# Order of the matmuls that sum a group of weighted rows: last-made row first, in a graph attention kernel on one Trainium2 core

## The chip, the core and the metric

The kernel runs on one core of one Trainium2 chip. The metric is the device time of an execution in microseconds (us); the time of a kernel is the median over its runs.

## What is computed

A node has 512 features; there are 3327 nodes (padded to 26 tiles of 128) and four layers of graph attention, each on a normalised input and added to it. Cut to one layer, the reference is:

```
h  = relu(layernorm(x)) @ W                      # 3327 x 512, in H heads of 512/H
e  = leaky_relu(s_src[i] + s_dst[j])             # for neighbours j of node i, per head
out_i = sum_j softmax_j(e_ij) * h_j
x  = x + out        (layers 1 and 2: x + elu(out))
```

Heads per layer: 8, 4, 1, 8. The neighbours come from an adjacency matrix with about 17 ones in a row, at most some 36.

## The kernel before

**Stage 0** (to about 317 us of the profiled execution) makes neighbour lists out of the adjacency matrix. Nodes are sorted by number of neighbours, so that tile 0 holds the nodes with most. `CAPS[t]`, 36 for tile 0 down to 11 for tile 25, is the number of neighbour slots of tile t.

**The layers** then work on lists (`tile_gat_lists`). Layer 0 takes all 26 tiles in that way, layer 1 tiles 1 to 25, layer 2 tiles 9 to 25, layer 3 tiles 3 to 25; the remaining tiles of layers 1 to 3, which have most neighbours, are done against all nodes with dense masked products (`Wholes`, L1153, and `Several`, L1301), laid between the list work. Layer l covers 317 to 1102 (l=0), 1130 to 1838 (l=1), 1838 to 2334 (l=2) and 2334 to 2972 us (l=3) of the profiled execution.

A tile's slots are cut into **groups** of up to four (`GROUP`); one group is one **step** s of a layer's list. The order on TensorE (PE), VectorE (DVE), ScalarE (ACT) and GpSimd (POOL) is written out by hand: within a step the pieces run as "first", then the scores of the next step, "scored", then `group` of this step, then "last". The steps of a group are these:

- `fetch` (POOL, L834): one indirect DMA for each slot gathers 128 rows of 528 numbers, each the features and scores of a neighbour, into `g[:, q, :]`. `gpool` has seven buffers, and fetches run up to seven steps ahead. A fetch into a buffer waits until DVE has read the group that was there.
- `scored` (DVE L887, L889, then ACT L890): scores of the four slots and their exponential, into `pw`. It runs one step ahead of `group`.
- `group` (DVE L918, PE L923): DVE multiplies each gathered row by its weights into `m[:, q, :]` (128x512, f32; `mpool` has three buffers), slot after slot. PE then sums the four products by matmuls with the identity matrix into the PSUM tile `self.po` ("bank"; two buffers). The first slot of a tile is not summed by PE: DVE writes its product straight into the bank. In layer 2 (one head) DVE does the sum itself (L911), without PE.
- A tile's last step s is followed by fixed later ones: `divisors` at s, `means` (L941, DVE reads the bank) and `added` (L961) two steps later, then `centre` (ACT L969), `turn` (PE transposes, L450), `cut` (ACT L457), `project` (PE L468), and `rows` (ACT L475 and a DMA of `v` to the table `tab`, from which the next layer gathers). The next layer's first gathers wait for the last of these.

A matmul of f32 appears in the trace as two records of PE, each with a weight load (PEld): 1207 matmuls in L923 are 2414 records. There are 356 groups with matmuls: 225 with four, 66 with three, 44 with two and 21 with one.

Of the kernel before, what the change touches and what calls it, by code (L numbers as in the profile page):

```python
# [795 lines left out]
def tile_gat_lists(ctx: ExitStack, tc: tile.TileContext, x, adj, ws, avs, out, ident, half, slots, L, low, spare, tabx, tabs):  # L796
# [7 lines left out]
    nc = tc.nc  # L804
# [40 lines left out]
    class Tile:  # L845
# [51 lines left out]
        def group(self, i):  # L897


            H, K, wt = HEADS[self.l], CAPS[self.t], self.wt  # L900
            D = F // H
            k0, n, g = self.groups[i]
            if H == 1:
                for q in range(n):
                    v = g[:, q, :].rearrange("p (s m) -> p s m", s=2)[:, :, :F // 2]
                    acc = self.po.rearrange("p (s m) -> p s m", s=2)
                    w = wt[:, k0 + q, 0:1]
                    if k0 + q == 0:
                        nc.vector.tensor_scalar(acc, v, w, None, OP.mult)
                    else:  # L910
                        nc.vector.scalar_tensor_tensor(acc, v, w, acc, OP.mult, OP.add)  # L911
                return
            m = pools["m"].tile([P, GROUP, F], F32, name="m")
            for q in range(n):
                v = g[:, q, :].rearrange("p (s m) -> p s m", s=2)[:, :, :F // 2]

                out_ = self.po if k0 + q == 0 else m[:, q, :]
                nc.vector.tensor_tensor(out_.rearrange("p (s h d) -> p s h d", s=2, d=D),  # L918
                                        v.rearrange("p s (h d) -> p s h d", d=D),
                                        wt[:, k0 + q, :H].rearrange("p (s h) -> p s h", s=2)  # L920
                                        .unsqueeze(3).to_broadcast([P, 2, H // 2, D]), OP.mult)
            for q in range(k0 == 0, n):
                nc.tensor.matmul(self.po, ident, m[:, q, :], start=False, stop=(k0 + q == K - 1),  # L923
                                 skip_group_check=True)

        def divisors(self):
# [542 lines left out]
```

## Time and profile before

| | |
|---|---|
| time, median of 3 runs | 2429.07 us (2425.39 to 2435.29) |
| span of the profiled execution | 2971.7 us, 27155 instructions |
| whole time of the profiled execution | not given beside its span |
| span less median | 542.6 us |
| PE busy | 2211.9 us, of which L923 1232.2 us |
| DVE busy | 1923.1 us, of which L918 into `m` 752.5 us |
| POOL busy | 1731.4 us |
| ACT busy | 934.6 us |
| mean granted clock of PE | 0.873 |

Busy times are from the profiler's records of one execution; a group is named by source line, engine and the tiles it writes and reads (`bank<-m,ident` is L923). "Idle before" is the time in which an engine did nothing ahead of an instruction, put down to whoever released it; "issue" is time for which the profile shows no such reason. The profiled execution took 22% longer than the median of the runs without it, so that its stretches can't be carried over one to one.

### The profile page before, as it was taken

The page shows a single profiled execution, that of the slowest core. Times are in us where ns is not written, and L with a number is a line of the kernel's source. Part 1 is how long each engine was busy: PE and PEld are TensorE (multiplying, and loading weights), DVE is VectorE, ACT ScalarE, POOL GpSimd, SP SyncE. Part 2 cuts the span into 40 slices and gives each one's busy share as a digit, 9 for nine tenths or more (in the row PEclk, how much of TensorE's full clock was granted, in tenths as well). Part 3 has the DMA queues.
Part 4 walks back from the last instruction along what each step waited for, and adds up shares of the span by engine and source line. Part 5 has one row for each costly group of instructions (what it writes and reads, how often), then busy time and mean ns, then how long its engine had stood idle before and what let it go on. Part 6 is the DMA issues. An engine that isn't in the chain of part 4 may idle for free.

```text
span 2971.7 us, 27155 instructions
## 1 busy us (share of the span) xinstructions
PE 2211.9 (74%) x7082; PEld 1246.1 (42%) x7082; DVE 1923.1 (65%) x4968; ACT 934.6 (31%) x2502; POOL 1731.4 (58%) x1717
## 2 busy tenths in 40 slices
PE   4777677776777764767777877588696688878887
PEld 2564233343433332434444444244354454545443
DVE  7987666655565533656665665598888366666665
ACT  5872122322221111322222322244333333323330
POOL 7885455565566635544556562676664556555653
PEclk9988888888898887988888898799898898989888
DMA  6885576786676756755667673787785566656663
GB/s 230 325 291 161 165 228 200 211 254 207 195 225 197 199 130 200 200 157 174 187 190 210 179 209 92 234 255 240 241 246 153 168 193 204 185 170 198 195 189 111
DMA packets 260731, 594.21 MB, mean 200 GB/s; under 512 B 103699, under 2 KB 121107, under 8 KB 256214
## 3 DMA queue, kind: packets, MB, share of 16 engines
q0 software_dynamic: 124368, 432.13, 49.8%
q1 hardware_dynamic: 132454, 153.45, 16.4%
q10 hardware_dynamic: 3744, 6.82, 0.7%
q8 instruction: 57, 0.93, 0.1%
q14 instruction: 108, 0.88, 0.1%
HBM read 542.60 MB, written 49.65 MB: 199 GB/s over the span
## 4 chain that ended last, share of the span: by engine, by line
PE 24%; DVE 18%; issue 14%; another core or an unknown queue 8%; ACT 5%; POOL 3%; DMA 2%; SPq 0%; DVEq 0%; POOLq 0%; ACTq 0%
PE bank L923 16%; DVE m L918 6%; PE pv L468 4%; PE whole L1301 3%; DVE bank L911 3%; POOL g L834 3%; ACT r L1267 1%; DVE z L889 1%; DVE z L887 1%; DVE x L961 1%; PE whole L1153 1%; DMA g<-tab,idxb 1%; DVE em L1126 1%; DVE q L438 1%
## 5 line engine op out<-in xcount | busy, mean ns | idle before, releaser
L923 PE MATMUL bank<-m,ident 128*128 128x512 f32 x2414 | 1232.2, 659 | 335.9 <-DVE m L918 197.3
L918 DVE TENSOR_TENSOR m<-g,pw 128x512 f32<-128x512 f32 x1207 | 752.5, 682 | 384.1 <-ACT pw L890 209.2
L834 POOL DMA_INDIRECT g<-tab,idxb x712 | 678.8, 953 | 482.0 <-issue 197.1
L923 PEld LDWEIGHTS bank<-m,ident 128*128 128x128 f32 x2414 | 488.8, 211 | 942.1 <-issue 582.4
L468 PE MATMUL pv<-w,hT 128*128 128x264 f32 x1664 | 434.9, 416 | 87.8 <-ACT hT L457 61.8
L834 POOL DMA_INDIRECT g<-tabx,twiceb x342 | 324.8, 950 | 230.7 <-issue 147.7
L834 POOL DMA_INDIRECT g<-tab,idxa x297 | 283.7, 955 | 248.4 <-issue 83.9
L468 PEld LDWEIGHTS pv<-w,hT 128*128 128x128 f32 x1664 | 334.1, 205 | 190.3 <-ACT hT L457 68.7
L890 ACT ACTIVATE pw<-z 128x32 f32<-128x32 f32 (+4 forms) x356 | 67.8, 191 | 850.7 <-DVE z L889 484.2
L1153 PE MATMUL whole<-ve,em 128*128 128x512 f32 x468 | 229.4, 642 | 54.1 <-issue 22.9
L1301 PE MATMUL whole<-L,room 128*128 128x130 f32 x1248 | 173.3, 290 | 59.9 <-issue 59.5
L1301 PEld LDWEIGHTS whole<-L,room 128*128 128x128 f32 x1248 | 164.7, 202 | 91.4 <-issue 89.7
L694 POOL TENSOR_TENSOR key<-a,keys 128x3328 int32<-128x3328 int32 (+1 forms) x29 | 189.3, 6530 | 16.3 <-DVE cand L703 11.8
L911 DVE SCALAR_TENSOR_TENSOR bank<-g,L,bank 128x512 f32<-128x512 f32 x243 | 183.3, 754 | 11.1 <-remote 2.0
L1153 PEld LDWEIGHTS whole<-ve,em 128*128 128x128 f32 x468 | 94.0, 206 | 167.4 <-issue 124.5
L834 POOL DMA_INDIRECT g<-tabx,twicea x99 | 94.7, 956 | 104.1 <-issue 51.1
L450 PE MATMUL pt<-ident,xn 128*128 128x128 f32 x416 | 70.8, 298 | 104.7 <-ACT xn L969 60.8
L703 DVE MAX8 cand<-key 128x8 f32<-128x208 int32 x416 | 144.3, 365 | 0.1
L475 ACT ACTIVATE v<-pv,rstd 128x528 f32<-128x528 f32 x78 | 54.2, 694 | 274.4 <-remote 126.5
L1267 ACT ACTIVATE r<-low,L 128x384 f32<-128x384 f32 x208 | 121.2, 583 | 16.9 <-remote 9.5
L918 DVE TENSOR_TENSOR bank<-g,pw 128x512 f32<-128x512 f32 x74 | 51.5, 696 | 100.7 <-ACT pw L890 69.2
L450 PEld LDWEIGHTS pt<-ident,xn 128*128 128x128 f32 x416 | 54.7, 153 | 144.4 <-ACT xn L969 69.1
(180 smaller groups left out, 2195.7 us busy)
## 6 DMA issues: line engine op xcount, KB each, us to landing
a<-in_adj SPq DMA_DIRECT2D x25, 1664.0 KB
tab<-v SPq DMA_DIRECT2D x78, 264.0 KB
ve<-tab SPq DMA_DIRECT2D x78, 264.0 KB
g<-tab SPq DMA_DIRECT2D x65, 264.0 KB
tabx<-vx SPq DMA_DIRECT2D x26, 528.0 KB
g<-tab,idxb POOLq DMA_INDIRECT x712
low<-tab SPq DMA_DIRECT2D x52, 132.0 KB
spare<-tab SPq DMA_DIRECT2D x52, 132.0 KB
```

The costliest lines, as they stand in the source:

```text
L450: nc.tensor.transpose(pt[:, k, :], xn[:, k * P:(k + 1) * P], ident)
L468: nc.tensor.matmul(pv[:, s, :HF + 8], hT[:, k, :], W.w[:, k, s, :], start=(k == 0), stop=(k == KC - 1))
L694: nc.gpsimd.tensor_tensor(key[:, c:c + quarter], a[:, c:c + quarter], keys[:, c:c + quarter], OP.mult)
L703: nc.vector.max(cand[:, g * 8:(g + 1) * 8], key[:, g * SEG:(g + 1) * SEG])
L834: nc.gpsimd.indirect_dma_start(out=out_, out_offset=None, in_=table, in_offset=bass.IndirectOffsetOnAxis(ap=which, axis=0))
L890: nc.scalar.activation(self.wt[:, k0:k0 + n, :H], z, AF.Exp)
L911: nc.vector.scalar_tensor_tensor(acc, v, w, acc, OP.mult, OP.add)
L918: nc.vector.tensor_tensor(out_.rearrange("p (s h d) -> p s h d", s=2, d=D), v.rearrange("p s (h d) -> p s h d", d=D), wt[:, k0 + q, :H].re ...
L923: nc.tensor.matmul(self.po, ident, m[:, q, :], start=False, stop=(k0 + q == K - 1), skip_group_check=True)
L1153: nc.tensor.matmul(tl.po.rearrange("p (s m) -> p s m", s=2), e[:, q * P:(q + 1) * P], v.rearrange("p (s m) -> p s m", s=2)[:, :, :F // 2], ...
L1267: nc.scalar.activation(self.r[:, h, :], self.a[:, g, :], AF.Relu, bias=-1.0, scale=self.b[:, j, g:g + 1])
L1301: nc.tensor.matmul(dst, e[:, h, q * P:(q + 1) * P], mov, start=False, stop=(j == NT - 1), skip_group_check=True)
```

## The change

The matmuls of a group are issued from the highest slot to the lowest. DVE still makes the products from the lowest slot to the highest. The `stop` mark moves to the matmul that now comes last in the tile's last group. Nothing else is changed; lines after L921 move down by one, so that the matmul's line becomes L924.

```
-            for q in range(k0 == 0, n):
-                nc.tensor.matmul(self.po, ident, m[:, q, :], start=False, stop=(k0 + q == K - 1),
+            first = int(k0 == 0)
+            for q in reversed(range(first, n)):
+                nc.tensor.matmul(self.po, ident, m[:, q, :], start=False, stop=(k0 + n == K and q == first),
                                  skip_group_check=True)
```

In the built program the first matmul of a group then waits for DVE's last product, and the others have no wait of their own. Over L923 the matmuls with a wait go from 1207 to 356 and those that signal a semaphore from 1151 to 392; of DVE's products (L918) those that signal go from 1278 to 1013, and those that wait stay 418. All other instructions keep their place on every engine.

## The prediction

> **What bounds the kernel now.** I read the busy times first, then those of each layer, the waits of PE and DVE, and a stretch of the timeline. The three costliest kinds of work are the page's top rows:
>
> ```profile
> span 2971.7 us, 27155 instructions
> ...
> L923 PE MATMUL bank<-m,ident 128*128 128x512 f32 x2414 | 1232.2, 659 | 335.9 <-DVE m L918 197.3
> L918 DVE TENSOR_TENSOR m<-g,pw 128x512 f32<-128x512 f32 x1207 | 752.5, 682 | 384.1 <-ACT pw L890 209.2
> L834 POOL DMA_INDIRECT g<-tab,idxb x712 | 678.8, 953 | 482.0 <-issue 197.1
> ```
>
> The changed matmuls are the largest row of all, and DVE's products are what most often ends PE's idleness. By layer (columns: window, its length, then PE, PEld, DVE, ACT, POOL busy, PE clock, DMA share, GB/s; layers 0, 1 and 3):
>
> ```profile
> 317.00:1102.00 785.00, 570.35 (x1617) 287.50 (x1616) 451.34 (x1189) 172.88 (x457) 455.33 (x479) 0.87 0.71 207
> 1130.00:1838.00 708.00, 542.92 (x1524) 286.56 (x1524) 441.25 (x1182) 195.16 (x595) 375.48 (x396) 0.87 0.63 181
> ...
> 2334.00:2972.00 638.00, 516.91 (x1976) 304.61 (x1976) 407.15 (x796) 195.75 (x610) 352.00 (x370) 0.89 0.63 181
> ```
>
> PE is busiest at 73 to 81%, so none is full. POOL's records hide that after each gather of 0.95 us it takes 0.30 us to issue the next. At 1.25 us a gather, 479, 396 and 370 of them are 600, 495 and 462 us, as much as PE's own 570, 543 and 517. The timeline of a clean stretch shows who sets the pace (start, length, engine, line; in brackets the idle time before):
>
> ```profile
> 928.63 2.48 DVE L918 TENSOR_TENSOR m<-g,pw 128x512 f32<-128x512 f32 x4 [0.33 <-issue]
> ...
> 928.96 0.95 POOL L834 DMA_INDIRECT g<-tabx,twiceb  x1 [0.30 <-issue]
> ...
> 929.37 3.70 PE L923 MATMUL bank<-m,ident 128*128 128x512 f32 x8 [1.08 <-issue]
> ...
> 930.21 0.95 POOL L834 DMA_INDIRECT g<-tabx,twiceb  x1 [0.30 <-issue]
> ```
>
> POOL is back to back, four gathers in 5.0 us. PE was idle for 1.08 us, starts 0.06 us after the first product (DVE makes one every 0.60 us), and runs its four matmuls at 0.86 us each behind the other three. This overlap of DVE and PE within one group is what the change gives up.
>
> ```profile
> PE bank L923 <- DVE m L918: 197.3, 68, 10.3
> ...
> DVE m L918 <- PE bank L923: 19.2, 17, 6.5
> ```
>
> PE waits for products far more than DVE waits for PE to free `m`: PE is usually drained, and DVE seldom blocked.
>
> **What the Trainium skill says.** "Perfetto Trace Analysis", section Tensor Engine Instruction: the end of a matmul's record is estimated, and its semaphore goes out only after PSUM has acknowledged the data. The trace agrees: records are 0.59 us long but start every 0.43 us, so I count starts, not lengths. "TensorE: Matmul & The Clock Gate", section The cost: per-tile semaphore tail: increments of matmuls that end together serialize at 26.3 ns each, and one on the last is enough, since matmuls end in order. No run here shows that price on matmuls that follow each other. The same page, HAM oscillation: gaps of over some 3.4 us drop PE to half clock. The trace shows it: after an idle 8.78 us at 617.9 us the records start every 0.86 us in place of 0.43.
>
> **The change part by part.**
> Waits: 1207 to 356, so 851 fewer. Price: starts of the two records within a matmul lie 429 ns apart (median), and from one matmul to the next, across wait and signal, also 429. A wait already met costs PE nothing: 0, with no gain to be had.
> Signals: 1151 to 392, so 759 fewer. By the same equality 0 on PE; the skill's price would make it at most 759 x 26.3 ns = 20 us, an estimate. I take 0 and keep -20.
> DVE's 265 fewer signals: products start every 598 ns with one and 605 without (three of these). 0.
> Start of a group: it moves from the first product's end to the last's, 3, 2 or 1 times 0.60 us later for four, three or two matmuls. If PE stood idle at each of the 225, 66 and 44 groups: 225 x 1.8 + 66 x 1.2 + 44 x 0.6 = 511 us. Comparing start by start in the trace, 193 of the 356 began before their last product was done, by 233 us together. Even that does not add up: PE takes its queue in order, so once it is 1.8 us late the next group's products are ready sooner relative to it. Shifting PE's rows so, all else held, its delay never passes 1.80 us, and at the ends of layers 0, 1 and 3 it is 0.13, 1.47 and 1.79 us, together +3.4 us. The last tiles have groups of one or two, hence the small first value. That is on the path: the next layer's gathers, or the end, wait for it.
> Behind the waiting matmul stand PE's transposes, projections (L468, 3.56 us) and dense products. Who waits for those? ACT's L475 and L457, with the next exponentials behind them on ACT, and DVE's means. They come two steps after the group, 10 us in a clean stretch, while PE is done 2.48 + 0.06 + 3.43 = 6.0 us after DVE began (4.2 now): 4 us to spare. Where steps bunch after a stall it is not so. I take +3 us for that.
> `m` coming free: slot 0 is now read last, so DVE's first write three groups on may begin 3 x 0.86 = 2.6 us later. On 17 waits that is at most 44 us of DVE idleness; two groups (6.9 us) are then in PE's hands, more than 2.6 + 0.6. At that moment PE hides it: 0. Without this cover it would be lost in full, with gathers behind it, though POOL is six groups ahead.
> No DMA is moved; POOL's and SP's queues keep their order.
> Sum on the profiled execution: 0 + 0 + 0 + 3.4 + 3 = +6 us on a span of 2971.7. The median is 542.6 us lower; the three layer ends are in it just as well, so I carry +6 over: 2435 us.
>
> **The rivals.**
> *Slower: drained hand-overs on the critical chain.* Following the chain of waits, it passes from a product to PE's matmuls at 29 places. For those whose first matmul preceded the last product the delays add to 40 us. If each closes a loop (PE late, ACT late, the next products late), the time is 2429 + 3 + 40 = 2472. It decides once more than some 6 of them count at 1.4 us each, with the layer ends. For it: PE's 197.3 us of waiting. Against: many follow stalls that an unprofiled execution may not have.
> *Faster: signals held up.* The trace has pauses in which PE's semaphores stand still and then arrive in a bunch:
>
> ```profile
> 616.32 0.70 ACT L475 ACTIVATE v<-pv,rstd 128x528 f32<-128x528 f32 x1 [13.36 <-remote]
> ```
>
> ACT waited for a projection recorded as done at 605.7, and PE's updates came at 616.1 to 616.5, 0.04 us apart. I count 64 such bunches, all in layers 0, 1 and 3, about one per 20 signals of PE, none in the 572 us around layer 2, where signals are rare. 542.6 / 64 = 8.5 us is the size of one, which suggests that the profiler makes them; then fewer signals shorten only the profiled execution. If the runs have them too, PE's signals fall by 759 of 2023 executed, 38%. Time with PE, DVE and ACT all idle for over 2 us sums to 210 us; 38% is 80 us, giving 2349.
> *Nothing happens:* the waits really fall, by the built program; but if PE is never drained in a run, its start moves nowhere and 2429 stays.
>
> **How the numbers follow.** Half a per cent (12 us) is about what a measurement can tell from no change. The shift of 3 to 9 us or none: 0.45, own range 2424 to 2441. Loops: 0.33, 2441 to 2480. Held-up signals or the skill's 20 us: 0.22, from 2300 to 2417. For 8 in 10 I reach to 2365 and 2480, leaving out most of the lower tail, about a tenth, and a few in a hundred above.
>
> **What would show it.** In the profile after: the first matmul of a group starts no earlier than 0.05 us after its last product, idleness of PE before it ended by L918 grows beyond 197 us, and spacing within a group stays 0.43 us per record. DVE's waits on PE for `m` stay below some 60 us, else cover has failed. Fewer bunches with an unchanged median says that they are the profiler's; with a median under 2417, that they are real. A median above 2441 says that loops close.

## The result and the profile after

The changed kernel takes 2460.77 us in the median of four runs (2457.97 to 2463.44), against 2430.45 for the kernel before (four runs, 2425.39 to 2435.29): a ratio of 1.0125, interval 1.0108 to 1.0142, so 30 us more. The profiled execution of after has a span of 2461.2 us and a whole time of 2462.9.

The kernel before takes 2430 us at some times and some 2970 at others, without a profile just as with one, and its profile in the prediction is of the second kind. That profile has the pauses in PE's signals that the prediction describes; the profile of after has none. So I set after against the fourth experiment, which takes the same 2430 us as before, has as many waits and signals on PE, and whose profile has no pauses either; I call it **the mirror**. First the rows of the page of after:

```profile
span 2461.2 us, 27155 instructions
...
L924 PE MATMUL bank<-m,ident 128*128 128x512 f32 x2414 | 1127.4, 613 | 155.8 <-DVE m L918 139.5
L834 POOL DMA_INDIRECT g<-tab,idxb x712 | 679.5, 954 | 253.2 <-issue 170.3
L918 DVE TENSOR_TENSOR m<-g,pw 128x512 f32<-128x512 f32 x1207 | 751.8, 681 | 130.1 <-ACT pw L890 126.4
```

and of the mirror, where the matmul's line is L925:

```profile
span 2429.7 us, 27155 instructions
...
L925 PE MATMUL bank<-m,ident 128*128 128x512 f32 x2414 | 1125.3, 614 | 120.1 <-DVE m L918 119.7
```

PE's work is the same to 2 us. DVE's products end 139.5 us of PE's idleness in place of 119.7. The pairs of the waits view for after (us in total, times, longest) add who does not wait:

```profile
PE bank L924 <- DVE m L918: 139.5, 100, 11.8
...
DVE bank L956 <- ACT ex L950: 21.1, 15, 4.1
...
DVE m L918 <- PE bank L924: 2.2, 2, 1.9
```

DVE waits for PE to free `m` for 2.2 us in all. A clean stretch of the timeline of after, in layer 0 (start, length, engine, line; idle time before in brackets), is the counterpart of the prediction's stretch at 928.63:

```profile
741.07 2.48 DVE L918 TENSOR_TENSOR m<-g,pw 128x512 f32<-128x512 f32 x4 [0.27 <-ACT pw L890]
...
743.60 7.13 PE L924 MATMUL bank<-m,ident 128*128 128x512 f32 x16 [0.97 <-DVE m L918]
...
744.15 2.48 DVE L918 TENSOR_TENSOR m<-g,pw 128x512 f32<-128x512 f32 x4 [0.31 <-ACT pw L890]
...
745.05 0.95 POOL L834 DMA_INDIRECT g<-tabx,twiceb  x1 [0.30 <-issue]
```

DVE's four products end at 743.55 and PE begins 0.05 us later, not beside them. Its 16 records are two groups: the second group's products were ready before PE came to them, so of two delays only one shows here.

Cut by layer, from DVE's first product into `m` to the end of its last (layer 2 has no matmul of L923, and is cut at its first and last sum on DVE, L911), the two profiled executions stand so:

| stretch, us | mirror | after | difference |
|---|---|---|---|
| stage 0, to the first product | 310.3 | 303.2 | -7.1 |
| layer 0 | 594.6 | 600.0 | +5.4 |
| from layer 0 to layer 1 | 39.8 | 42.5 | +2.7 |
| layer 1 | 519.6 | 540.4 | +20.8 |
| from layer 1 to layer 2 | 34.3 | 36.8 | +2.5 |
| layer 2 | 417.6 | 417.6 | 0 |
| from layer 2 to layer 3 | 33.1 | 33.0 | -0.1 |
| layer 3 | 469.2 | 474.9 | +5.7 |
| last product to the end | 11.2 | 12.9 | +1.7 |
| span | 2429.7 | 2461.2 | +31.5 |

Stage 0, which the change does not touch, scatters by 9 us between executions (301.4 to 310.3 in the traces of after and experiments 1 to 4), so a single row is good to some us, and the rows below stage 0 add to 38.6 us, more than the 30.3 us of the timed runs; these carry the verdicts. Layer 1 stands out. That the mirror may stand for the kernel before can be seen in experiments 1 to 3: the layers that they leave in the order of before take 595 and 596 us (layer 0), 522 and 521 (layer 1) and 469.2 twice (layer 3) in their traces, within 3 us of the mirror's.

### The profile page after: what moved, and what is told of

The parts are those of the page before. It is cut to its first block, busy times and chain, and to the rows that moved or that the text cites. A ratio compares the mean times of both kernels' runs of the same rounds, so it can differ in the third digit from the quotient of the medians.

```text
span 2461.2 us, 27155 instructions
## 1 busy us (share of the span) xinstructions
PE 2062.4 (84%) x7082; PEld 1181.7 (48%) x7082; DVE 1926.0 (78%) x4968; ACT 932.3 (38%) x2502; POOL 1733.0 (70%) x1717
## 3 DMA queue, kind: packets, MB, share of 16 engines
q1 hardware_dynamic: 132454, 153.45, 19.2%
## 5 line engine op out<-in xcount | busy, mean ns | idle before, releaser
L924 PE MATMUL bank<-m,ident 128*128 128x512 f32 x2414 | 1127.4, 613 | 155.8 <-DVE m L918 139.5
L918 DVE TENSOR_TENSOR m<-g,pw 128x512 f32<-128x512 f32 x1207 | 751.8, 681 | 130.1 <-ACT pw L890 126.4
L924 PEld LDWEIGHTS bank<-m,ident 128*128 128x128 f32 x2414 | 449.9, 195 | 694.6 <-issue 467.1
L468 PE MATMUL pv<-w,hT 128*128 128x264 f32 x1664 | 435.5, 416 | 70.7 <-ACT hT L457 44.7
L468 PEld LDWEIGHTS pv<-w,hT 128*128 128x128 f32 x1664 | 334.7, 205 | 172.8 <-ACT hT L457 51.1
L911 DVE SCALAR_TENSOR_TENSOR bank<-g,L,bank 128x512 f32<-128x512 f32 x243 | 183.2, 754 | 6.8
L1302 PEld LDWEIGHTS whole<-L,room 128*128 128x128 f32 x1248 | 147.5, 190 | 24.9 <-issue 23.7
L1302 PE MATMUL whole<-L,room 128*128 128x130 f32 x1248 | 147.8, 274 | 0.0
L887 DVE TENSOR_TENSOR z<-g,pw 128x32 f32<-128x32 f32 (+4 forms) x356 | 61.8, 174 | 71.5 <-DMA g<-tab,idxa 38.5
L1120 ACT ACTIVATE r<-low,mc,b 128x384 f32<-128x384 f32 x78 | 52.6, 674 | 155.3 <-DVE em L1127 132.3
```

The costliest lines, as they stand in the source:

```text
L468: nc.tensor.matmul(pv[:, s, :HF + 8], hT[:, k, :], W.w[:, k, s, :], start=(k == 0), stop=(k == KC - 1))
L887: nc.vector.tensor_tensor(z, g[:, :n, ROW - 8:ROW - 8 + H], self.s.unsqueeze(1).to_broadcast([P, n, H]), OP.add)
L1302: nc.tensor.matmul(dst, e[:, h, q * P:(q + 1) * P], mov, start=False, stop=(j == NT - 1), skip_group_check=True)
```

## The experiments

Each experiment is compared with the kernel before, timed beside it on the same chip: 2429.99 us for 1 to 4, 2971.1 for 5 to 8, 2969.97 for 9 and 10, 2999.38 for 11 and 2972.46 for 12. So 1 to 4 show what happens without the pauses, 5 to 12 what happens with them. Lines below L921 stand one higher in the experiments than in after (L925 for L924, L1280 for L1279).

### 1 to 3: the reversal in one layer alone

```
-            for q in range(k0 == 0, n):
+            order_ = list(range(int(k0 == 0), n))
+            order_ = order_[::-1] if self.l == 0 else order_     # 1; == 1 in 2, == 3 in 3
+            for q in order_:
```

with the `stop` mark on the last of `order_`. Expected:

> The reversed order in layer 0 alone, the order of before in layers 1 and 3. Theory A (the gathers of POOL pace layers 0 and 3; a late PE costs only where it comes back to stop POOL, and at layer ends): POOL was back to back through nearly all of layer 0 in the profile after, so +3 to +8 us over before. Rival B (every group met by an idle PE loses a bit on a closed loop, evenly): 133 of 356 groups, so 133/356 of 30 us = +11 us. Rival C (reading the buffer or the bank in another order, or fewer signals, is itself slower, whatever the start): also +11 us.

> The reversed order in layer 1 alone. Theory A: layer 1 is the one where POOL stood waiting for DVE (some 33 us between 1054 and 1290 us of the profile after), so most of the 30 us: +15 to +25 us over before. Rivals B and C: 118 of 356 groups, +10 us.

> The reversed order in layer 3 alone. Theory A: POOL had one gap over 0.45 us in all of layer 3 after, so only the end of the layer, +2 to +4 us over before. Rivals B and C: 105 of 356 groups, +9 us.

Measured: layer 0 alone 2433.62 us, ratio 1.0015 (1.0008 to 1.0022), +3.6 us; layer 1 alone 2449.42, 1.0081 (1.0066 to 1.0097), +19.4; layer 3 alone 2437.41, 1.0024 (1.0014 to 1.0035), +7.4. The sum, 30.4 us, is the 30.3 of the whole change: no interaction of the layers shows, and two thirds of the loss lie in layer 1. Layers 0 and 1 came as the expectation's theory A had them. Layer 3 did not: it lost 7.4 us, where A gave it 2 to 4 for the end of the layer and the evenly spread rivals 9. In its trace the stretch of layer 3 itself grows by 6.3 us against the mirror, 2.4 of them at the second groups of tiles and 1.8 at the fifth; what holds these groups was not tested.

Why layer 1? One tile of it in the mirror's timeline:

```profile
1254.15 1.88 DVE L918 TENSOR_TENSOR m<-g,pw 128x512 f32<-128x512 f32 x3
...
1254.88 2.84 PE L925 MATMUL bank<-m,ident 128*128 128x512 f32 x6 [0.90 <-DVE m L918]
...
1257.56 3.72 PE L468 MATMUL pv<-w,hT 128*128 128x264 f32 x16
...
1261.12 0.61 PE L1303 MATMUL whole<-low 128*128 128x129 f32 x4
...
1261.55 0.69 ACT L1280 ACTIVATE low<-low 128x128 f32<-128x128 f32 x2 [0.30 <-PE whole L1303]
...
1264.25 0.69 DVE L957 SCALAR_TENSOR_TENSOR bank<-ex,bank 128x512 f32<-128x512 f32 x1 [1.18 <-ACT ex L951]
...
1266.44 2.48 DVE L918 TENSOR_TENSOR m<-g,pw 128x512 f32<-128x512 f32 x4 [0.25 <-ACT pw L890]
```

and the same tile in the run with layer 1 reversed:

```profile
1259.60 1.88 DVE L918 TENSOR_TENSOR m<-g,pw 128x512 f32<-128x512 f32 x3
...
1261.53 2.84 PE L925 MATMUL bank<-m,ident 128*128 128x512 f32 x6 [1.99 <-DVE m L918]
...
1264.21 3.72 PE L468 MATMUL pv<-w,hT 128*128 128x264 f32 x16
...
1267.77 0.61 PE L1303 MATMUL whole<-low 128*128 128x129 f32 x4
...
1268.19 0.70 ACT L1280 ACTIVATE low<-low 128x128 f32<-128x128 f32 x2 [1.50 <-PE whole L1303]
...
1269.03 0.68 ACT L475 ACTIVATE v<-pv,rstd 128x528 f32<-128x528 f32 x1
...
1270.89 0.70 DVE L957 SCALAR_TENSOR_TENSOR bank<-ex,bank 128x512 f32<-128x512 f32 x1 [2.38 <-ACT ex L951]
...
1273.09 2.48 DVE L918 TENSOR_TENSOR m<-g,pw 128x512 f32<-128x512 f32 x4 [0.25 <-ACT pw L890]
```

Count from each fence's first line. PE starts this group's three matmuls after 0.73 us and after 1.93: 1.20 later, two products of 0.60. The projection (L468) starts at 3.41 and 4.61, ACT's copy of a dense tile's result (L1280) at 7.40 and 8.59, DVE's ELU (L957) at 10.10 and 11.29, and the first products behind it at 12.29 and 13.49. The 1.20 us goes whole through PE, ACT and DVE into the next products. No link of this tile has anything to spare: already in the mirror ACT waits 0.30 us for PE and DVE 1.18 us for ACT. The idle times grow by the same 1.2.

Set product by product against each other over all of layer 1, these two executions part by 18.2 us, of which 10.9 come at the fourth group of a tile, the first after the ELU of the tile before, in steps that are mostly near 1.2 us: 1.20 for tile 11, then 1.26, 1.20, 1.19, 1.23, 1.47 and 0.80 for tiles 10, 9, 7, 6, 5 and 3, and 1.8 for tile 13. So eight of the layer's 25 tiles show the step; of the rest, 4.5 us come at first groups and 3.1 at fifth groups. The waits of layer 1 show the links, first the mirror (944 to 1470 us), then the run with layer 1 reversed (938 to 1483):

```profile
DVE ve L979 <- ACT waste L974: 13.7, 13, 2.5
...
DVE bank L957 <- ACT ex L951: 7.0, 11, 1.2
...
DVE den L1321 <- PE whole L1303: 1.4, 1, 1.4
```

```profile
DVE ve L979 <- ACT waste L974: 18.4, 14, 3.1
DVE bank L957 <- ACT ex L951: 18.0, 15, 2.4
...
DVE den L1321 <- PE whole L1303: 6.1, 2, 4.3
```

DVE's wait for ELU's exponential rises by 11.0 us in sum, its waits for ACT's squares and for the dense product by 4.7 each.

In layer 0 the delay is largely given back. Product by product, after loses 11.7 us against the mirror at the tiles' first groups and 3.8 at the fourth, and gains 8 back at the fifth and sixth. The stretches of each layer (window, length, then PE, PEld, DVE, ACT and POOL busy, PE clock, DMA share, GB/s; layers 0, 1 and 3) suggest who takes over, first for the mirror, then for after:

```profile
309.00:909.00 600.00, 530.81 (x1619) 272.44 (x1617) 452.79 (x1190) 173.77 (x458) 446.12 (x470) 0.96 0.87 264
944.00:1470.00 526.00, 490.41 (x1524) 267.53 (x1524) 442.11 (x1182) 193.36 (x597) 375.22 (x396) 0.98 0.82 244
1948.00:2429.00 481.00, 461.67 (x1976) 278.88 (x1976) 408.31 (x799) 193.60 (x613) 355.70 (x375) 0.98 0.81 243
```

```profile
303.00:910.00 607.00, 526.71 (x1618) 268.36 (x1616) 451.94 (x1191) 174.44 (x457) 449.04 (x472) 0.97 0.87 261
945.00:1494.00 549.00, 499.69 (x1524) 270.25 (x1524) 441.48 (x1183) 195.48 (x597) 375.77 (x396) 0.97 0.79 233
1973.00:2461.00 488.00, 461.13 (x1976) 277.12 (x1976) 407.30 (x796) 193.23 (x610) 356.63 (x374) 0.99 0.80 239
```

At 1.25 us a gather (0.95 us and 0.30 to the next, as above), the mirror's 470 of layer 0 are 588 of 600 us, and its 396 of layer 1 only 495 of 526; in after they are 590 of 607 and 495 of 549. In layer 0 POOL sets the pace nearly throughout and a late group can catch up with it; in layer 1 it has 31 us of slack even before the loss, and the ring of PE, ACT and DVE sets the pace instead. Layer 3 fits less well: there POOL has 12 us of slack in the mirror (375 gathers, 469 of 481 us), as in layer 0, and the loss is twice that of layer 0. That POOL's slack is why the layers differ is read from these numbers and was not varied by itself.

### 4: DVE's products reversed as well (the mirror)

```
-            for q in range(n):
+            for q in [0] * (k0 == 0) + list(reversed(range(int(k0 == 0), n))):
                 ...                       # DVE's product of slot q
...
-            for q in range(k0 == 0, n):
+            order_ = list(range(int(k0 == 0), n))
+            order_ = order_[::-1]
+            for q in order_:
```

The product that goes straight to the bank is still made first. PE takes the slots in the changed kernel's order, but again each as soon as it is made; 1207 matmuls wait and 1151 signal, as before.

> DVE's products of a group are made in reversed order too (the bank's own product first), so that PE again meets the first-made product first; waits and signals are 1207 and 1151 as before. Theory A and rival B (it is the start of PE behind the last product): the time of before, within 5 us. Rival C (the order in memory, or the bank's order of additions, costs): stays at +30 us.

Measured: 2430.04 us, ratio 0.9999 (0.9991 to 1.0008). The loss is gone. So it isn't the order of the sum, the order in which PE reads the buffer or the moved `stop` mark; it is that PE asks for the last-made product first. In the mirror's trace some 185 groups begin before their last product ends, by 217 us together; in after none, the first matmul starting 0.05 us or more after it. The mirror brings the waits and signals of before back together with the early start, so by itself it does not part the two. Against the rival that fewer waits or signals are slower in themselves speak the uneven shares of experiments 1 to 3, PE's spacing (0.43 us from record to record in after and in the mirror alike) and the 1.20 us of the tile above, which is two products' time.

### 5, 6, 9 and 12: layer 1's reversal cut by place in the tile

```
+            order_ = order_[::-1] if self.l == 1 and i == 0 else order_    # 5, 9, 12: a tile's first group
+            order_ = order_[::-1] if self.l == 1 and i > 0 else order_     # 6: all other groups
```

> The reversed order only in the first group of each tile of layer 1 (25 groups with three matmuls; 1.2 us of start each), all else as before. Theory A, by the traces: in layer 1 the delay is taken up tile by tile on one loop (first group's sums, then projection L468 and dense products on PE, then the copies and the exponential of ELU on ACT, then DVE's L956 and the next products), so +12 to +18 us of the 19 us of layer 1. Rival D (any group's late start counts alike; shares by the sum of start delays, 25 x 1.2 = 30 us of 173 us in layer 1): +3.4 us.

> The complement: the reversed order in all groups of layer 1 but the first of each tile. Theory A: +2 to +7 us, the end of the layer above all. Rival D: +16 us (143 us of 173 us of start delay).

> As e5, because the chip of e5 to e8 was one on which the kernel before takes 2971 us and its trace shows PE's completions held up every 30 us or so, so that the loop of layer 1 was not what limited it. On a chip without such pauses (before at about 2430 us): theory A +12 to +18 us, rival D +3.4 us. On a chip with them: within 10 us, which tells nothing of the two.

> The kernel of e5 once more, for a chip on which before takes about 2430 us: theory A +12 to +18 us (in the trace of e2, layer 1's growth over the undelayed order comes in steps of 1.2 us, the delay of a first group of three, 10.9 of 18.2 us of it at the step of DVE's L956), rival D +3.4 us. On a chip on which before takes about 2970 us: within 10 us, as in e5 and e9.

Measured, all with the pauses: first groups 2974.50, 2971.40 and 2972.76 us, ratios 1.0010 (0.9989 to 1.0030), 1.0022 (0.9994 to 1.0050) and 1.0023 (0.9992 to 1.0055), each interval with 1 in it; the other groups 2977.66 us, 1.0046 (1.0022 to 1.0071). The other groups cost something there. For the first groups no loss is clear of the scatter, and theory A's 12 to 18 us did not come; since the intervals of experiments 5 and 6 overlap, it isn't shown which cost more. The theories were worked out from traces without pauses, and which groups cost the 19.4 us there was not measured.

### 7, 8, 10 and 11: ELU's exponential moved ahead of the scores on ACT

In layer 1 the two ACT instructions of ELU (L948, L950) are put first in their place of the hand-written order, in the changed kernel (7, 10, 11) and in the kernel before (8), so that DVE's L956 finds its operand done:

```
-        at.setdefault((s, place), []).append(piece)
+        row = at.setdefault((s, place), [])
+        early = getattr(piece, "__name__", "") == "bent" and piece.__self__.l == 1
+        row.insert(0 if early else len(row), piece)
```

> The changed kernel with one piece moved on ACT: in layer 1 the two instructions of ELU (L948, L950) go ahead of the dense features (L1279, which wait for PE) and of the copy of the projection (L475, which waits for PE). DVE's L956 then waits for nothing that PE is late with. Theory A: most of layer 1's 19 us comes back, 2442 to 2450 us. Rival E (the late freeing of the product buffers or DVE's other waits carry the delay): 2458 to 2462 us.

> The same move in the kernel before. Theory A: DVE's wait for ELU's exponential was 8 us in 12 places of layer 1 with PE starting early, so -3 to -10 us. Rival E: no change, within 4 us of before.

> As e7, for the same reason. On a chip without pauses: theory A 2442 to 2450 us, rival E 2458 to 2462 us. On a chip with them: about +1% over before again.

> The kernel of e7 once more, for a chip on which before takes about 2430 us. There theory A says 2442 to 2450 us (the delay of layer 1 came back to DVE through ELU's exponential), rival E 2458 to 2462 us. On a chip on which before takes about 2970 us: +1% over before, as in e7 and e10.

Measured, again with the pauses: the changed kernel so moved takes 2998.70, 2997.22 and 3017.42 us, ratios to before 1.0104 (1.0076 to 1.0133), 1.0087 (1.0057 to 1.0117) and 1.0076 (1.0046 to 1.0105); the kernel before so moved 2960.26, 0.9962 (0.9945 to 0.9978), 11 us less. With the same move on both sides the reversal of all three layers costs 38 us (2998.70 less 2960.26); in the two traces layer 1 is longer by 11.8 us and layer 0 by 15.2. The move takes DVE's wait for `ex` out of layer 1: it is 41.8 us in the trace of before, in six waits of up to 13.1 us, and a single wait of 1.3 us in those of experiments 7 and 8. A loss thus remains with that wait gone. What the reversal costs with the pauses but without the move was not timed, so whether the move gave part of it back is open; and waits of that length are not the steps of 1.2 us that make up the loss without pauses. For those the link through `ex` stays read from the timeline, not shown by taking it away. Whether experiment 8 also gains at 2430 us was not measured.

These runs also bear on the rival of the held-up signals. Take as a bunch four or more updates of PE's semaphore in a row, each less than 0.08 us after the one before. The trace of before has 64, experiments 5, 6 and 8 have 59, 48 and 62, experiment 7 has 26; after and experiments 1 to 4 have none. The lines of the waits view of experiment 8 look like the prediction's 13.36 us on ACT:

```profile
ACT v L475 <- remote: 156.2, 12, 27.1
...
ACT low L1280 <- remote: 85.9, 13, 22.0
```

The bunches go with the times near 2970 us, which runs without a profile show as well, so they are not the profiler's. And fewer signals brought no net gain: experiment 7, with 26 bunches in place of 62, is 38 us slower than experiment 8. The pauses themselves fell less than the bunches, for which four signals have to meet: from the first product on, PE, DVE and ACT are all idle for over 2 us at 34 places (162 us together) in experiment 7 and at 38 (182 us) in experiment 8.

## Where the prediction was right and where wrong

2460.77 us lies in the range, but 26 us above the predicted time and outside the likeliest case's own 2424 to 2441. What happened is the rival that was given 0.33. The range holds because it was drawn wide enough for that rival; the sum behind 2435 us does not hold.

**Waits and signals: 0, right.** In after PE's records still start every 0.43 us (16 in 7.13 us above), with 356 waits as with 1207, and no row of the table but stage 0 is shorter by more than 0.1 us. The chance of -20 us for the signals shows nowhere; a small gain hidden under the loss can't be told from the times alone.

**Start of a group: right in kind and size.** None starts before its last product, and in the tile above the delay is 1.20 us for three matmuls. In places it came to more, where PE's clock fell behind the longer idleness. The same tile in after:

```profile
1267.54 1.87 DVE L918 TENSOR_TENSOR m<-g,pw 128x512 f32<-128x512 f32 x3
...
1269.47 4.54 PE L924 MATMUL bank<-m,ident 128*128 128x512 f32 x6 [1.98 <-DVE m L918]
...
1280.53 0.70 DVE L956 SCALAR_TENSOR_TENSOR bank<-ex,bank 128x512 f32<-128x512 f32 x1 [4.08 <-ACT ex L950]
...
1282.72 2.48 DVE L918 TENSOR_TENSOR m<-g,pw 128x512 f32<-128x512 f32 x4 [0.25 <-ACT pw L890]
```

Six records take 4.54 us here in place of 2.84, being partly at half clock, so that the next products come 15.18 us after the first line in place of 12.29: 1.2 + 1.7 us more. Layer 1 of after has eight half-clock stretches (27 us together), the mirror three (14 us) and experiment 2 five (17 us). The prediction quoted the half clock and priced none of it. Over the whole kernel it does not add up to a cost: from 300 us on, half clock takes 211 us in after and 217 in the mirror, since layer 0 has 27 us of it in after and 45 in the mirror.

**Layer ends: +3.4 predicted, 6.9 in the table.** The two with a delay of 1.47 and 1.79 came as 2.5 and 1.7; the first, put at 0.13, came as 2.7, and 2.1 in experiment 1 against the mean of three traces in which layer 0 is not delayed (41.7 against 39.6).

**Who waits for what stands behind the matmul: this is the step that failed.** The prediction had "4 us to spare", and took "+3 us" where it is not so. Of 30.3 us measured, some 6.9 are ends by the table; the remaining 23 or so stand in that term's place. Two things went wrong in it. The slack was counted in one clean stretch of layer 0, where POOL is full, and applied to layer 1, which has other consumers (the dense products L1302 with ACT's L1279 behind them) and, in the tile shown, no room at all. And the shift of PE's rows was made "all else held", which by its making can't show a loop: the delay never passed 1.80 us because DVE's products were kept in place, when in fact they came later by it in tile after tile.

**`m` coming free: 0, right.** DVE waits 2.2 us for it, against 2.4 in the mirror, so the later reading of slot 0 costs nothing that shows. The 19.2 us of the trace of before are gone in both, along with the pauses.

**"PE idleness ended by L918 grows beyond 197 us": failed as a sign.** It is 139.5 us, since the pauses of the trace of before are absent. Against the mirror it grew, from 119.7.

**The rival that happened** is drained hand-overs on the critical chain, 43 us predicted and 30 found. What was put against it, that many follow stalls which an unprofiled execution may not have, was wrong: 193 groups began before their last product in the trace with pauses, and some 185 do in the mirror's without. That the two sums lie near each other is in part luck: the 40 us were read from a chain with pauses in it. The reading of the pauses, "which suggests that the profiler makes them", fell with experiments 5 to 12, where runs without a profile took some 2970 us too. So did the carrying over: +6 was worked out in an execution with the pauses and added to a median without them.

**What stays open:** which of layer 1's groups carry the loss where before takes 2430 us; whether freeing one link (ELU, or ACT's copies of the dense products) would give it back there; where layer 3's 7.4 us come from; and what causes the pauses.

## What to carry to other kernels

A consumer that asks for the last-made operand first gives up the overlap within the group, and where waits already met cost nothing there is no gain to set against it. Count the slack of what stands behind a delayed instruction in the stage with the least, not in the clean stretch at hand, and follow it once round: a shift "all else held" shows delays but no loops, and the waits of the other engines for one another (here DVE's for ACT, whose own line waits for PE) tell whether a loop is closed. When span and median differ by a fifth, as here, the profile's waits need a second trace before they are weighed.

## What the runs showed of the hardware

The expectations of experiments 9 to 12 took the pauses for a property of the chip. They are not tied to the chip's number: the results name number 6 for experiments 1 to 4, which have none, as for 5 to 8, which have them, and numbers 14, 0 and 2 for the others that have them. Whether one number is one and the same chip is not on record. In the traces with pauses stage 0 is little longer (313 to 323 us against 301 to 310), and so is layer 2, with few signals of PE (428 to 438 us against 418 to 422), while layers 0, 1 and 3, cut as above, take 781.6, 700.8 and 626.5 us in the trace of before against 594.6, 519.6 and 469.2 in the mirror. The mean granted clock is 0.873 there against 0.941, a step of 7% where the layers are 31 to 35% longer; at full clock PE's records start 0.43 us apart in both. I read the rest as the pauses of PE's signals, which no run took away by themselves.

On the half clock, the Trainium skill ("TensorE: Matmul & The Clock Gate", section HAM oscillation) speaks of gaps of over some 3.4 us. This case's traces do not agree with that as a rule for the last gap. At the tile above PE was idle for 1.98 us in after and 1.99 in experiment 2; the first was followed by a half-clock stretch, the second was not. And the longest gap of PE in the 10 us before each of the eight half-clock stretches in layer 1 of after is 1.9 to 3.2 us. So the length of the last gap alone does not decide it, and half clock comes behind gaps well under 3.4 us too.
